# Layer 0's second norm as a node factor on ScalarE, and its keys, values and context moved beside the checks

## The chip, the core and the metric

The kernel runs on one core of one Trainium2 chip. The metric is the device time of one launch in microseconds (us), median over the runs shown; lower is better.

## The reference, cut to what matters

A graph of 3,125 nodes with 256 features and 103,125 edges, sorted by destination, goes through four layers. Each layer is a norm, a graph attention over the edges, a dense linear attention ("mix") over all nodes, and a feed-forward part. Only the front of layer 0 is touched by the change:

```python
xn = _layernorm(x)                                  # first norm
x = x + _L0_gnn_ref(xn, edge_index, ...) + _L0_mix_ref(xn[None], ...)[0]

def _L0_mix_ref(x, Wqkv, Wproj, bproj, ln_g, ln_b, Wg1, bg1, Wg2, bg2):
    q, k, v = split((x @ Wqkv))                     # 8 heads of 32
    k = softmax(k, axis=1)                          # over the nodes
    context = einsum('bnhd,bnhv->bhdv', k, v)
    out = einsum('bnhd,bhdv->bnhv', q, context)
    xn = (x - mean(x)) * rsqrt(var(x) + 1e-05) * ln_g + ln_b   # second norm, of a normed x
    hgate = gelu(xn @ Wg1 + bg1)
    gate = sigmoid(hgate @ Wg2 + bg2)
    return out * gate @ Wproj + bproj
```

The second norm is taken of rows that are normed already: their mean is 0 and their variance is v/(v + 1e-5), where v is the variance of the row of x. Its result is therefore the first norm's row times one number of that node.

## The kernel before, in words

Nodes lie in 25 tiles of 125 rows (`NT`, `TP`), and these in seven `GROUPS` of four or three tiles (500 or 375 nodes). `x` and the normed `xn` stay in SBUF by rows, `xT` holds the normed features transposed (two blocks of 128, `KC`).

`run` has these stages, one after the other:

1. **The begin** (`begin_layer`): `x` is loaded; for every group VectorE takes `bn_stats`/`bn_aggr` of each tile, ScalarE the square root, VectorE the reciprocal and the scaling (L613 to L619); TensorE transposes the tiles (L288), and ScalarE and VectorE copy them out to `xT` (L294, L296).
2. **The checks** (`prepare`): they establish whether the edges have the form that the fast path needs. `heads_i` (1.6 MB) is loaded, five comparisons over 3,224 numbers (L1381) give `at_i`, with which GpSimd gathers `seg` (L1387); VectorE works that into `lo` and `key` and writes both to `seg_d` in DRAM (L1392 to L1404); `dst_i` is compared (L1419 to L1428); TensorE multiplies `xT` with a 16-column matrix, and VectorE takes the largest and the least (`p_e`, `ends`, L1438, L1439). One number, `self.ok`, is the outcome, and all engines branch on it (L2479). Nothing behind the branch can run before it.
3. **The counts** (`counts`), with **layer 0's mix** beside them: `lo` and `key` are read back (`seg_in`), transposed by TensorE and copied out as `lo_t` and `key_t`. Then come 63 steps of ten groups of nodes. A step makes two one-hot tiles on VectorE (`oh_lo` L1515, `oh_key` L1518), 20 matmuls of them on TensorE (`p_cnt`, L1530), and ScalarE copies the counts out as bytes (`stage`, L1532). Every 250 nodes a stage goes to `count_d` in DRAM (L1536).
4. **The pairs** (`dense_pairs`): 25 x 8 x 2 passes that read `count_d` back as `a` (L1706) and bound VectorE and TensorE for over 300 us. The other layers follow.

The mix is a generator, `mix0_pieces`, which gives the control back after each piece of work; after each step of the counts as many pieces are issued as keep pace with `PIECES0` pieces over the 63 steps, and what is left follows behind the loop. The pieces before are: one for the weights and the bias (`nc.gpsimd.tensor_add` over all of `x`, L1557); 25 for the tiles' keys and values (four matmul instructions into `p_a` at L716, `ek` = exp of the keys at L1564 and `v` at L1566 on ScalarE, a column of ones by GpSimd at L1567, four matmul instructions into `p_ctx` at L1569); one that folds the context into the query weights (`ctxt`, `fold`, L1575 to L1587); then six for each group: second norm `xnn` (L613 to L619 again), transposes and scaling `xnnT` (L1599, L1600), `hg`, `gate`, the product with `fold` (L1616), the projection added to `x` (L1623); then 38 of `node_pieces`, which make the node tables `zs`, `bar`, `q_g` that the pairs use. That is 1 + 25 + 1 + 42 + 38 = 107.

The order of each engine's instructions is settled at build time by the tile framework: earlier emitted instructions have the higher priority, but one that its estimates hold ready may be put ahead of one that waits. [...] DMAs are issued from the queues of SP and ScalarE; GpSimd issues the gathers.

Of the kernel before, what the change touches and what calls it, by code (L numbers as in the profile page):

```python
# [10 lines left out]
F32 = mybir.dt.float32  # L11
# [30 lines left out]
KEYS = HI * GN  # L42
PIECES0 = 107
SC = 8
# [12 lines left out]
class Net:  # L57
# [546 lines left out]

    def layernorm(self, out, src, group=None):

        nc = self.nc
        w = self.norms
        for t0, nt in GROUPS if group is None else [group]:
            mv = w.tile([TP, 4, 2], F32, name="mv")  # L610
            for t in range(nt):
                st = w.tile([TP, nc.vector.BN_STATS_DIM], F32, name="bn_st")
                nc.vector.bn_stats(st, src[:, t0 + t, :])  # L613
                nc.vector.bn_aggr(mv[:, t, :], st)
            rstd = w.tile([TP, 4], F32, name="rstd")
            nc.scalar.activation(rstd[:, :nt], mv[:, :nt, 1], AF.Sqrt, bias=self.eps5[:TP], scale=1.0)
            nc.vector.reciprocal(rstd[:, :nt], rstd[:, :nt])
# [112 lines left out]
    def mix0(self, x, xn, xT):  # L730
        nc, tc = self.nc, self.tc
        with ExitStack() as s:
# [9 lines left out]
            bg1, bg2 = self.vec(c, "L0_mix_bg1", rows=64), self.vec(c, "L0_mix_bg2")  # L742
            bproj = self.row(c, "L0_mix_bproj", parts=1)
            gate = c.tile([P, KC, N], F32, name="gate")
# [53 lines left out]
            for t0, nt in GROUPS:  # L798
# [11 lines left out]
                for t in range(nt):  # L810
                    p = ps.tile([TP, C], F32, name="p_a")
                    self.mm(p, [(og[:, m, t * TP:(t + 1) * TP], wproj[:, m, :]) for m in range(KC)]
                            + [(self.ones[:1, :TP], bproj)])
                    nc.vector.tensor_add(x[:, t0 + t, :], x[:, t0 + t, :], p)
# [536 lines left out]
class Dense(Net):  # L1351
# [8 lines left out]
    def prepare(self, pool, xT):  # L1360
# [6 lines left out]
        with ExitStack() as s:  # L1367
# [65 lines left out]
            gw = self.gnn_weight(w, ps, "g0", 8)  # L1433
            ends = w.tile([16, 2, len(GROUPS)], F32, name="ends")
# [30 lines left out]
            nc.vector.tensor_mul(self.ok, ok[:, 0:1], ok[:, 2:3])  # L1465
        return self.ok

# [4 lines left out]
    def counts(self, pieces):  # L1472
# [5 lines left out]
        with ExitStack() as s:  # L1478
# [5 lines left out]
            with tc.tile_pool(name="cnti", bufs=1) as wi, tc.tile_pool(name="cntt", bufs=2, space=PSUM) as ps:  # L1484
                for i, name in enumerate(("lo_t", "key_t")):
# [57 lines left out]
    def mix0_pieces(self, x, xn, xT, nodes, c, w):  # L1543


        nc, tc = self.nc, self.tc
        with ExitStack() as s:
            ps = s.enter_context(tc.tile_pool(name="m0p", bufs=3, space=PSUM))
            ps1 = s.enter_context(tc.tile_pool(name="m0p1", bufs=1, space=PSUM))
            wqkv = self.weight(c, "L0_mix_Wqkv")  # L1550
            wproj = self.weight(c, "L0_mix_Wproj")
# [3 lines left out]
            bg1, bg2 = self.vec(c, "L0_mix_bg1", rows=64), self.vec(c, "L0_mix_bg2")  # L1555
            bproj = self.row(c, "L0_mix_bproj")
            nc.gpsimd.tensor_add(x, x, bproj[:, None, :].to_broadcast([TP, NT, C]))  # L1557
            p_ctx = [ps1.tile([P, P + 1], F32, name=f"p_ctx{m}") for m in range(KC)]
            yield
            for t in range(NT):  # L1560
                p = ps.tile([TP, 2 * C], F32, name="p_a")
                self.mm(p, [(xT[:, k, t * TP:(t + 1) * TP], wqkv[:, k, C:]) for k in range(KC)])
                ek = w.tile([TP, C], F32, name="ek", bufs=2)
                nc.scalar.activation(ek, p[:, :C], AF.Exp)  # L1564
                v = w.tile([TP, KC, P + 1], F32, name="v", bufs=2)
                nc.scalar.activation(v[:, :, :P], p[:, C:].rearrange("p (m f) -> p m f", m=KC), AF.Copy)  # L1566
                nc.gpsimd.memset(v[:, :, P], 1.0)  # L1567
                for m in range(KC):
                    nc.tensor.matmul(p_ctx[m], ek[:, m * P:(m + 1) * P], v[:, m, :], start=(t == 0), stop=(t == NT - 1))  # L1569
                yield  # L1570

            inv = w.tile([P, KC], F32, name="inv")
            ctxt = w.tile([P, KC, P], F32, name="ctxt")
            for m in range(KC):
                nc.vector.reciprocal(inv[:, m:m + 1], p_ctx[m][:, P:])  # L1575
                nc.vector.scalar_tensor_tensor(ctxt[:, m, :], p_ctx[m][:, :P], inv[:, m:m + 1], self.heads, op0=OP.mult, op1=OP.mult)
            fold = c.tile([P, KC, C], F32, name="fold")
            for k in range(KC):
                p = ps.tile([P, 512], F32, name="p_a")
                for m in range(KC):  # L1580
                    nc.tensor.transpose(p[:, m * P:(m + 1) * P], wqkv[:, k, m * P:(m + 1) * P], self.ident)
                wt = w.tile([P, C], F32, name="wq_t")
                nc.vector.tensor_copy(wt, p[:, :C])
                p = ps.tile([P, 512], F32, name="p_a")
                for m in range(KC):
                    nc.tensor.matmul(p[:, m * P:(m + 1) * P], wt[:, m * P:(m + 1) * P], ctxt[:, m, :], start=True, stop=True)
                nc.vector.tensor_copy(fold[:, k, :], p[:, :C])  # L1587
            yield
            for t0, nt in GROUPS:
                n = nt * TP  # L1590
                cs = slice(t0 * TP, t0 * TP + n)
                xnn = w.tile([TP, 4, C], F32, name="xnn")
                self.layernorm(xnn, xn[:, t0:t0 + nt, :], (0, nt))
                yield
                xnnT = w.tile([P, KC, 512], F32, name="xnnT")
                for k in range(KC):
                    p = ps.tile([P, 512], F32, name="p_a")
                    for t in range(nt):
                        nc.tensor.transpose(p[:, t * TP:(t + 1) * TP], xnn[:, t, k * P:(k + 1) * P], self.ident[:TP, :TP])  # L1599
                    nc.vector.tensor_scalar(xnnT[:, k, :n], p[:, :n], g[:, k:k + 1], b[:, k:k + 1], op0=OP.mult, op1=OP.add)  # L1600
                yield
# [864 lines left out]
    def run(self, x_in, out):  # L2466
# [195 lines left out]
```

## Time and profile before

| what | us |
|---|---|
| median of 3 runs (lowest, highest) | 5535.72 (5531.63, 5546.36) |
| the profiled execution: its own time | 5533.53 |
| its span in the trace | 5531.5 |
| begin and checks, until `ok` is written | 0 to 92.3 |
| from there to the first count matmul | 92.3 to 130.5 |
| the 63 steps | 130.5 to 384.7 |
| last copy of counts to the first matmul of the pairs | 384.7 to 408.2 |

The span is one execution on the core, and all stages are read from it. A row of windows gives the busy time of each engine in a stretch, with the number of instructions; "busy" of TensorE (PE) is the union of its matmuls. PEclk is the clock granted to it, as a share of full speed. In a group of instructions the columns are line, engine, operation, output <- inputs, shapes and count, then busy us and mean ns of one, then the engine's idle time before them and what ended it. A mean of a matmul is longer than the distance between two of them, since they overlap.

### The profile page before, as it was taken

What the parts mean: (1) busy time and instruction counts of PE and PEld (TensorE: products, weight loads), DVE (VectorE), ACT (ScalarE), POOL (GpSimd) and SP (SyncE); (2) the same over time, 40 slices, a digit from 0 to 9 for tenths busy, and PEclk for the clock granted to TensorE, in tenths of its full rate; (3) what the DMA queues carried; (4) which work ended last, traced back from release to release, by engine and by line L of the source; (5) the groups of instructions that cost most, each with busy time, mean ns of one, the idle gap of its engine ahead of it and who ended that gap; (6) DMA issues with size and microseconds to landing.
All of it is one profiled execution on the core that took longest, in us unless ns stands there. A gap on an engine that the chain in (4) does not pass through costs nothing. (4 is left out here: it accounts for less than half of the span.)

```text
span 5531.5 us, 66568 instructions
## 1 busy us (share of the span) xinstructions
PE 4813.9 (87%) x24758; PEld 2824.0 (51%) x24758; DVE 3733.4 (67%) x5901; ACT 1034.3 (19%) x1984; POOL 1041.6 (19%) x1185
## 2 busy tenths in 40 slices
PE   4978888879788899989889899979998878989878
PEld 2652234448645433368544433345565555655557
DVE  7789999985565699845333899932223888777753
ACT  2540010011142100110123000023333110333221
POOL 1000000004300000000001100000001777777743
PEclk7999999989899999999889999979999888999989
DMA  3462222232300011111000011120002556666645
GB/s 87 36 68 67 77 63 67 67 116 63 99 19 0 27 34 41 32 39 36 24 1 4 28 33 34 26 71 0 0 1 59 161 164 193 183 173 178 175 149 170
DMA packets 294339, 395.81 MB, mean 72 GB/s; under 512 B 124175, under 2 KB 228000, under 8 KB 293435
## 3 DMA queue, kind: packets, MB, share of 16 engines
q1 hardware_dynamic: 203408, 161.12, 12.7%
q0 software_dynamic: 52528, 167.17, 10.7%
q10 hardware_dynamic: 38072, 63.16, 3.6%
q8 instruction: 202, 3.31, 0.3%
q14 instruction: 129, 1.06, 0.1%
HBM read 345.14 MB, written 49.35 MB: 71 GB/s over the span
## 5 line engine op out<-in xcount | busy, mean ns | idle before, releaser
L1699 DVE SCALAR_TENSOR_TENSOR pt<-q_head,bar,a 128x750 f32<-128x750 f32 (+5 forms) x1200 | 1483.3, 1298 | 80.4 <-PE acc L1804 57.3
L1954 POOL DMA_INDIRECT z_edge<-tab,src_i x806 | 778.0, 965 | 266.9 <-issue 206.4
L1748 PE MATMUL acc<-pt,zs 128*64 128x500 f32 (+2 forms) x2800 | 591.1, 548 | 152.0 <-DVE pt L1699 127.2
L1799 PE MATMUL acc<-pt,zs 128*64 128x375 f32 (+2 forms) x3200 | 604.9, 501 | 25.4 <-DVE pt L1699 25.0
L2022 PE MATMUL p_acc<-z_edge,oh 128*125 128x264 f32 x2044 | 539.9, 425 | 91.7 <-DVE z_edge L2013 91.7
L2022 PEld LDWEIGHTS p_acc<-z_edge,oh 128*125 128x125 f32 x2044 | 419.8, 209 | 191.3 <-DVE z_edge L2013 101.2
L1748 PEld LDWEIGHTS acc<-pt,zs 128*64 128x64 f32 (+1 forms) x2800 | 244.4, 136 | 483.3 <-DVE pt L1699 328.7
L1799 PEld LDWEIGHTS acc<-pt,zs 128*64 128x64 f32 (+1 forms) x3200 | 244.9, 136 | 362.0 <-issue 224.7
L1215 DVE SCALAR_TENSOR_TENSOR x<-p_y,sm,x 125x256 f32<-125x256 f32 x200 | 93.9, 484 | 427.0 <-PE p_y L716 427.0
L1804 PE MATMUL acc<-pt,zs 128*32 128x375 f32 (+2 forms) x3200 | 313.4, 497 | 0.0
L1850 PE MATMUL acc<-zs,pt 128*125 128x257 f32 x1250 | 275.7, 383 | 11.8 <-DMA a<-count_d 11.8
L1850 PEld LDWEIGHTS acc<-zs,pt 128*125 128x125 f32 x1250 | 234.8, 189 | 52.7 <-issue 14.6
L2013 DVE TENSOR_TENSOR z_edge<-z_edge,near_e 128x2112 f32<-128x2112 f32 (+1 forms) x101 | 236.5, 2342 | 17.4 <-ACT near_e L2005 17.4
L1210 ACT ACTIVATE h<-p_tr,bn 128x500 f32<-128x500 f32 (+1 forms) x224 | 161.5, 722 | 357.6 <-PE p_tr L716 357.6
L716 PE MATMUL p_y<-w_L_ffn_Wo,h 128*125 128x256 f32 x800 | 203.7, 387 | 0.0
L1699 DVE SCALAR_TENSOR_TENSOR pt<-q_all,bar,a 128x500 f32<-128x500 f32 (+3 forms) x175 | 119.0, 682 | 122.9 <-PE acc L1850 120.4
L716 PE MATMUL p_tr<-h,w_L_ffn_W 128*128 128x500 f32 (+1 forms) x448 | 191.6, 551 | 7.8 <-ACT h L1210 4.7
L2362 POOL CAST one_e<-one 125x96 bf16<-125x96 f32 (+1 forms) x2 | 2.1, 1049 | 1013.5 <-DVE one L653 1013.5
L716 PE MATMUL p_tr<-xT,w_L_ffn_W 128*128 128x500 f32 (+1 forms) x448 | 190.0, 547 | 0.0
L1804 PEld LDWEIGHTS acc<-pt,zs 128*32 128x32 f32 (+1 forms) x3200 | 85.0, 109 | 203.0 <-issue 201.7
L716 PEld LDWEIGHTS p_y<-w_L_ffn_Wo,h 128*125 128x125 f32 x800 | 144.9, 187 | 73.4 <-ACT h L1210 27.1
L1967 DVE TENSOR_TENSOR hot<-row,near 125x1024 f32<-125x1024 int16 (+1 forms) x149 | 157.6, 1083 | 4.5 <-DMA row<-dst_row 2.9
(513 smaller groups left out, 6696.0 us busy)
## 6 DMA issues: line engine op xcount, KB each, us to landing
row<-dst_row SPq DMA_DIRECT2D x101, 224.0 KB
a<-count_d SPq DMA_DIRECT2D x96, 203.1 KB
a<-count_d SPq DMA_DIRECT2D x96, 187.5 KB
a<-count_d SPq DMA_DIRECT2D x144, 93.8 KB
ef<-in_edge_s SPq DMA_DIRECT2D x101, 128.0 KB
z_edge<-tab,src_i POOLq DMA_INDIRECT x806
count_d<-stage SPq DMA_DIRECT2D x12, 781.2 KB
q_head<-q_g ACTq DMA_DIRECT2D x24, 375.0 KB
```

The source lines that it names most:

```text
L716: self.nc.tensor.matmul(p, a, b, start=(i == 0), stop=(i == len(pairs) - 1))
L1210: nc.scalar.activation(o[:, m, :n], p[:, :n], AF.Relu, bias=b[:, e, m:m + 1], scale=g[:, e, m:m + 1])
L1215: nc.vector.scalar_tensor_tensor(x[:, t0 + t, :], q, wf[:, t, e:e + 1], x[:, t0 + t, :], op0=OP.mult, op1=OP.add)
L1699: self.nc.vector.scalar_tensor_tensor(pt[:K, :n], q, bar, a[:K, :n], op0=OP.max, op1=OP.mult)
L1748: nc.tensor.matmul(acc[64 * i:64 * i + 64, :b1 - b0], zs[:K, t, z:z + 64], pts[i][:K, b0:b1], start=(t == 0), stop=(t == NS - 1))
L1799: nc.tensor.matmul(acc[i // 2][64 * (i % 2):64 * (i % 2) + 64, b, :b1 - b0], zs[:K, t, i * W:i * W + 64], pts[i][:K, b0:b1], **st)
L1804: nc.tensor.matmul(acc[2][32 * i:32 * i + 32, b, :b1 - b0], zs[:K, t, z:z + 32], pts[i][:K, b0:b1], **st)
L1850: nc.tensor.matmul(acc[i], pt[:K, i * TP:(i + 1) * TP], zs[:K, t, :C + 1], start=(t == 0), stop=(t == NS - 1))
L1954: nc.gpsimd.indirect_dma_start(out=zs[i][:, j, :], out_offset=None, in_=table, in_offset=bass.IndirectOffsetOnAxis(ap=src[:, c0 + j:c0 + j ...
L1967: nc.vector.tensor_tensor(hots[i, t][:, q0 * 256:q1 * 256], rows[i][:, q0 * 256:q1 * 256], node[:, t:t + 1].to_broadcast([TP, (q1 - q0) * ...
L2013: nc.vector.tensor_mul(zh, zh, weight[:, :, :, None].to_broadcast([P, n, H, D + 1]))
L2022: nc.tensor.matmul(acc[t], ohs[i, t][:, k - a, :], zs[i][:, k - c0, :HW], start=(k == cols[t][0]), stop=(k == cols[t][1] - 1))
```

## The change

The begin, the checks and the first half of the mix become one function, `begin`; `prepare` turns into a generator with two stops. The second norm's statistics are not taken any more: `layernorm` is given `again`, in which it leaves the factor of each node, and `mix0_pieces` multiplies by it on ScalarE; `xnnT` is made on ScalarE too. The bias is added in `begin`. `fold` goes through DRAM (`fold_d`) from one stage to the other. `bproj` also goes out of `mix0`, which runs only in the general branch.

```diff
-PIECES0 = 107
+PIECES0 = 69
 def layernorm(self, out, src, group=None, again=None):
             nc.scalar.activation(rstd[:, :nt], mv[:, :nt, 1], AF.Sqrt, bias=self.eps5[:TP], scale=1.0)
+            if again is not None:
+                twice = w.tile([TP, 4], F32, name="twice")
+                nc.scalar.activation(twice[:, :nt], mv[:, :nt, 1], AF.Sqrt, bias=self.eps10[:TP], scale=1.0 + 1e-5)
+                nc.vector.reciprocal(twice[:, :nt], twice[:, :nt])
+                nc.vector.tensor_mul(again[:, t0:t0 + nt], twice[:, :nt], rstd[:, :nt])
...
 def prepare(self, pool, xT):
...                                    (gathers of seg)
+            yield
...                                    (seg to lo, key, found; dst)
+            yield
-            p_f = ps.tile([1, 2], F32, name="p_f")
+            p_f = ps.tile([1, 2], F32, name="p_e")
...                                    (p_e, ends, w_k, ok)
+    def begin(self, pool, x, xn, xT):
+        self.fold_d = self.dram.tile([P, KC * C], F32, name="fold_d")
...                                    (pools: c0w bufs=2; PSUM c0t 2, c0p 2, c0c 1)
+            checks = self.prepare(pool, xT)
+            next(checks)
+            wqkv = self.weight(c, "L0_mix_Wqkv")
+            p_ctx = [ps1.tile([P, P + 1], F32, name=f"p_ctx{m}") for m in range(KC)]
+            self.again = pool.tile([TP, NT], F32, name="again")
+            self.layernorm(xn, x, GROUPS[0], self.again)
+            for i, (t0, nt) in enumerate(GROUPS):
+                self.transposed(pst, xT, xn, groups=[GROUPS[i]])
+                if i + 1 < len(GROUPS):
+                    self.layernorm(xn, x, GROUPS[i + 1], self.again)
+                if i == 2:
+                    next(checks)
+                for t in range(t0, t0 + nt):
...                                    (p_a, ek, v, ones, p_ctx: as in mix0_pieces before)
+            bproj = self.row(c, "L0_mix_bproj")
+            nc.gpsimd.tensor_add(x, x, bproj[:, None, :].to_broadcast([TP, NT, C]))
...                                    (inv, ctxt, fold: as in mix0_pieces before)
+            nc.sync.dma_start(self.fold_d, fold.rearrange("p k f -> p (k f)"))
+            for _ in checks:
+                pass
 def counts(self, pieces):
-            ps = s.enter_context(tc.tile_pool(name="cntp", bufs=3, space=PSUM))
+            ps = s.enter_context(tc.tile_pool(name="cntp", bufs=4, space=PSUM))
 def mix0_pieces(self, x, xn, xT, nodes, c, w):
-            ps = s.enter_context(tc.tile_pool(name="m0p", bufs=3, space=PSUM))
-            ps1 = s.enter_context(tc.tile_pool(name="m0p1", bufs=1, space=PSUM))
-            wqkv = self.weight(c, "L0_mix_Wqkv")
+            ps = s.enter_context(tc.tile_pool(name="m0p", bufs=4, space=PSUM))
-            bproj = self.row(c, "L0_mix_bproj")
-            nc.gpsimd.tensor_add(x, x, bproj[:, None, :].to_broadcast([TP, NT, C]))
...                                    (25 pieces of keys and values, one of the context: gone)
             fold = c.tile([P, KC, C], F32, name="fold")
+            nc.sync.dma_start(fold.rearrange("p k f -> p (k f)"), self.fold_d)
             yield
...
-                self.layernorm(xnn, xn[:, t0:t0 + nt, :], (0, nt))
+                for t in range(nt):
+                    nc.scalar.activation(xnn[:, t, :], xn[:, t0 + t, :], AF.Copy, scale=self.again[:, t0 + t:t0 + t + 1])
...
-                    nc.vector.tensor_scalar(xnnT[:, k, :n], p[:, :n], g[:, k:k + 1], b[:, k:k + 1], op0=OP.mult, op1=OP.add)
+                    nc.scalar.activation(xnnT[:, k, :n], p[:, :n], AF.Identity, bias=b[:, k:k + 1], scale=g[:, k:k + 1])
 def run(self, x_in, out):
-        self.begin_layer(x, xn, xT)
-        ok = nc.values_load(self.prepare(pool, xT)[0:1, 0:1], min_val=0, max_val=1)
+        self.begin(pool, x, xn, xT)
+        ok = nc.values_load(self.ok[0:1, 0:1], min_val=0, max_val=1)
```

The pieces after are 1 + 42 + 38 = 81, of which 69 are spread over the 63 steps and the last twelve follow behind the loop.

More of the change, by code (lines that the diff above doesn't have):

```diff
@@ L603, in experts, with layernorm @@
         return t
-    def layernorm(self, out, src, group=None):
+    def layernorm(self, out, src, group=None, again=None):
         nc = self.nc
@@ L742, in mix0 @@
             bg1, bg2 = self.vec(c, "L0_mix_bg1", rows=64), self.vec(c, "L0_mix_bg2")
-            bproj = self.row(c, "L0_mix_bproj", parts=1)
             gate = c.tile([P, KC, N], F32, name="gate")
@@ L811, in mix0 @@
                     p = ps.tile([TP, C], F32, name="p_a")
-                    self.mm(p, [(og[:, m, t * TP:(t + 1) * TP], wproj[:, m, :]) for m in range(KC)]
-                            + [(self.ones[:1, :TP], bproj)])
+                    self.mm(p, [(og[:, m, t * TP:(t + 1) * TP], wproj[:, m, :]) for m in range(KC)])
                     nc.vector.tensor_add(x[:, t0 + t, :], x[:, t0 + t, :], p)
@@ L1428, in prepare @@
             nc.vector.tensor_reduce(found[:, 1:2], above, AX.X, OP.add)
-            p_f = ps.tile([1, 2], F32, name="p_f")
+            yield
+            p_f = ps.tile([1, 2], F32, name="p_e")
             nc.tensor.matmul(p_f, self.ones[:, 0:1], found, start=True, stop=True)
-            gw = self.gnn_weight(w, ps, "g0", 8)
+            gw = self.gnn_weight(w, ps, "g0", 8, "p_e")
             ends = w.tile([16, 2, len(GROUPS)], F32, name="ends")
@@ L1465, in prepare @@
             nc.vector.tensor_mul(self.ok, ok[:, 0:1], ok[:, 2:3])
-        return self.ok
+    def begin(self, pool, x, xn, xT):
+        nc, tc = self.nc, self.tc
+        self.fold_d = self.dram.tile([P, KC * C], F32, name="fold_d")
+        with ExitStack() as s:
+            c = s.enter_context(tc.tile_pool(name="c0", bufs=1))
+            w = s.enter_context(tc.tile_pool(name="c0w", bufs=2))
+            pst = s.enter_context(tc.tile_pool(name="c0t", bufs=2, space=PSUM))
+            ps = s.enter_context(tc.tile_pool(name="c0p", bufs=2, space=PSUM))
+            ps1 = s.enter_context(tc.tile_pool(name="c0c", bufs=1, space=PSUM))
+            checks = self.prepare(pool, xT)
[11 more added lines that the diff above has]
+                for t in range(t0, t0 + nt):
+                    p = ps.tile([TP, 2 * C], F32, name="p_a")
+                    self.mm(p, [(xT[:, k, t * TP:(t + 1) * TP], wqkv[:, k, C:]) for k in range(KC)])
+                    ek = w.tile([TP, C], F32, name="ek")
+                    nc.scalar.activation(ek, p[:, :C], AF.Exp)
+                    v = w.tile([TP, KC, P + 1], F32, name="v")
+                    nc.scalar.activation(v[:, :, :P], p[:, C:].rearrange("p (m f) -> p m f", m=KC), AF.Copy)
+                    nc.gpsimd.memset(v[:, :, P], 1.0)
+                    for m in range(KC):
+                        nc.tensor.matmul(p_ctx[m], ek[:, m * P:(m + 1) * P], v[:, m, :], start=(t == 0), stop=(t == NT - 1))
+            bproj = self.row(c, "L0_mix_bproj")
+            nc.gpsimd.tensor_add(x, x, bproj[:, None, :].to_broadcast([TP, NT, C]))
+            inv = c.tile([P, KC], F32, name="inv")
+            ctxt = c.tile([P, KC, P], F32, name="ctxt")
+            for m in range(KC):
+                nc.vector.reciprocal(inv[:, m:m + 1], p_ctx[m][:, P:])
+                nc.vector.scalar_tensor_tensor(ctxt[:, m, :], p_ctx[m][:, :P], inv[:, m:m + 1], self.heads, op0=OP.mult, op1=OP.mult)
+            fold = c.tile([P, KC, C], F32, name="fold")
+            for k in range(KC):
+                p = ps.tile([P, 512], F32, name="p_a")
+                for m in range(KC):
+                    nc.tensor.transpose(p[:, m * P:(m + 1) * P], wqkv[:, k, m * P:(m + 1) * P], self.ident)
+                wt = w.tile([P, C], F32, name="wq_t")
+                nc.vector.tensor_copy(wt, p[:, :C])
+                p = ps.tile([P, 512], F32, name="p_a")
+                for m in range(KC):
+                    nc.tensor.matmul(p[:, m * P:(m + 1) * P], wt[:, m * P:(m + 1) * P], ctxt[:, m, :], start=True, stop=True)
+                nc.vector.tensor_copy(fold[:, k, :], p[:, :C])
+            nc.sync.dma_start(self.fold_d, fold.rearrange("p k f -> p (k f)"))
+            for _ in checks:
+                pass
@@ L1555, in mix0_pieces @@
             bg1, bg2 = self.vec(c, "L0_mix_bg1", rows=64), self.vec(c, "L0_mix_bg2")
-            bproj = self.row(c, "L0_mix_bproj")
[L1557 to L1576, printed above, removed]
-            fold = c.tile([P, KC, C], F32, name="fold")
[L1578 to L1587, printed above, removed]
+            fold = c.tile([P, KC, C], F32, name="fold")
+            nc.sync.dma_start(fold.rearrange("p k f -> p (k f)"), self.fold_d)
             yield
```

## The prediction

> **What bounds the kernel now.** Only the first 408 us are touched, so I read the table of windows first, for who is busy when.
>
> ```profile
> 0.00:60.00 60.00, 18.22 (x69) 11.21 (x70) 48.99 (x123) 6.94 (x15) 8.65 (x62) 0.74 0.45 108
> 60.00:120.00 60.00, 22.72 (x61) 7.93 (x58) 43.85 (x97) 8.54 (x21) 15.10 (x7) 0.71 0.32 89
> 120.00:180.00 60.00, 56.36 (x401) 38.70 (x402) 42.16 (x39) 36.36 (x85) 4.46 (x21) 0.95 0.38 32
> 240.00:300.00 60.00, 56.62 (x361) 37.13 (x362) 51.20 (x58) 33.23 (x56) 0.00 (x0) 0.94 0.54 37
> ```
>
> The columns are length, PE, weight loads, DVE, ACT, POOL, PE clock. Begin and checks (to 92.3) belong to VectorE: 49 us of the first 60, with PE at 18. In the counts PE is busy 94%, VectorE 70 to 85%. The same question by groups of instructions, for the startup of the counts (93 to 131 us):
>
> ```profile
> L1557 POOL TENSOR_TENSOR x<-x,r_L_mix_bproj 125x6400 f32<-125x6400 f32 x1 | 13.7, 13682 | 12.8 <-DMA r_L_mix_bproj<-in_L_mix_bproj 12.8
> L1518 DVE TENSOR_TENSOR oh_key<-key_t,is_key 128x2520 bf16<-128x2520 bf16 x2 | 11.7, 5892 | 3.5 <-ACT key_t L1497 3.5
> L1569 PE MATMUL p_ctx<-v,ek 125*128 125x129 f32 x16 | 3.5, 359 | 7.5 <-POOL v L1567 7.5
> ```
>
> The bias addition holds GpSimd 13.7 us; behind it waits the memset of `v`, behind that `p_ctx` on PE (7.5 us), and two `oh_key` take 11.7 us instead of 2.9. So the first count matmul comes at 130.5. And for the steps (131 to 384 us):
>
> ```profile
> L1530 PE MATMUL p_cnt<-oh_key,oh_lo 128*128 128x125 bf16 x1245 | 91.6, 226 | 5.7 <-DVE oh_key L1518 4.5 <-ACT stage L1532 0.4 <-ACT zs L1665 0.4
> L1515 DVE TENSOR_TENSOR oh_lo<-lo_t,is_lo 128x2560 bf16<-128x2560 bf16 x60 | 89.3, 1489 | 30.5 <-PE p_cnt L1530 29.5
> L1518 DVE TENSOR_TENSOR oh_key<-key_t,is_key 128x2520 bf16<-128x2520 bf16 x60 | 87.8, 1464 | 0.0
> ...
> L716 PE MATMUL p_a<-w_L_mix_Wqkv,xT 128*125 128x512 f32 x74 | 35.6, 600 | 0.0
> ...
> L1569 PE MATMUL p_ctx<-v,ek 125*128 125x129 f32 x84 | 14.0, 290 | 1.6 <-ACT v L1566 1.0
> ```
>
> VectorE waits 29.5 us for PE to free one-hot buffers, PE only 5.7 before the counts: PE bounds the steps. The timeline gives the distance between two 512-column passes with the clock up, and the end of the stage:
>
> ```profile
> 125.70 0.19 PEld L716 LDWEIGHTS p_a<-w_L_mix_Wqkv,xT 128*125 128x125 f32 x1 [0.41 <-issue]
> ...
> 126.13 0.19 PEld L716 LDWEIGHTS p_a<-w_L_mix_Wqkv,xT 128*125 128x125 f32 x1 [0.24 <-issue]
> ...
> 400.94 12.88 SPq L1706 DMA_DIRECT2D a<-count_d  x5
> ...
> 408.15 7.04 PE L1748 MATMUL acc<-pt,zs 128*64 128x500 f32 x20 [24.32 <-DMA a<-count_d]
> ```
>
> 0.43 us a pass; and the pairs start 23.5 us after the last counts (384.7), because the last DMA to `count_d` has to land first.
>
> [...] The windows show 0.50 from 35 to 55 us, and 1.00 in the steps.
>
> **Part 1, the begin grows.** To PE goes: per tile four passes at 0.43 plus 0.61 for the four `p_ctx` (timeline, 129.13) = 2.33 us, for 25 tiles 58; fold 2.4 (rows L1581, L1586: 0.8 + 1.6). Its own there: transposes 11.2, of which I count 6 after 27 us; `p_e` 16 x 0.42 + 12 x 0.32 = 10.5 (0.43 scaled by columns); the rest 2.
> When can it start? `wqkv` (768 KB) now stands on SP behind `x` and `heads_i`: x 3.2 + heads 1.6 + dst 0.4 + wqkv 0.8 = 6.0 MB at the 259 to 272 GB/s of the windows 7 to 21 us is 23 us, plus some for the loads of `gw`: about 27 us. `x` is normed by then up to group 3 or so; `heads_i` lands about then too, its comparisons (17.8 + 1.8) have priority and delay the last groups, but PE has 9 us of work in every group.
> PE then ends at 27 + 6 + 58 + 2.4 + 10.5 + 2 = 106, and I add 2 for the clock to come up, and 5 for `ctxt`, copies and the chain to `ok` (2.6 in the trace, from 89.66). So `ok` at **113 instead of 92.3: +21**.
> VectorE isn't the bound: about 70 us now (windows to 93), plus 7 x 2 x 0.17 for the factor and 2.6 for the context = 75 from 7 us. It even loses a wait: `at_i` is ready some 10 us earlier, and the 7.4 us until `seg` lands are filled with norms. ScalarE gets 25 x 2 x 0.39 = 19.5, 7 x 0.3 for the second roots and a pair of table loads (2.6) wherever exp and sqrt alternate, at most 18: 40 of 85 us.
> GpSimd: 25 memsets, the five gathers (7.2 us) and the bias (13.7) share one list; a memset behind one of the latter holds `p_ctx` for up to that time less two tiles ahead (4.7), so 0 to 12 us, in which `p_e` can run on PE. I take 0. `bproj`'s load on ScalarE's queue, `fold_d`'s write on SP (0.26 MB) and its load after the branch cost nothing as long as VectorE or PE work: `fold` is wanted five pieces later. Bounds: +8 (PE's moved work in gaps that I don't see, `wqkv` at 20 us) to +40 (both POOL waits, all table loads).
>
> **Part 2, the startup of the counts shrinks.** Gone are the bias, the 25 `bn_stats` (9.6, which ran while VectorE waited for `key_t` anyway, so worth nothing), the load of `wqkv` and 26 passes plus 16 `p_ctx` in front of the last `seg_in` transposes. What stays is the chain: ten loads, two at a time, about 4 us each (99.2, 101.5, 106.6 in the timeline), `key_t` the sixth, then 3 us of one-hots: 18 to 22 us after the branch. I take 20 instead of 38.2: with the 1 us to the branch **-17** (-12 to -20).
>
> **Part 3, the steps shrink.** PE: windows 131 to 384 sum to 241.8; minus 35.6, 14.0 and 2.4 is 190, minus seven node tiles that go behind the loop (25.6/24 each) 182. VectorE: two one-hots 1.40 apart by the timeline, 63 steps 175; gate products, additions to `x` and `es` 18: 193. Its `xnn` (7.3) and `xnnT` (9.7) go to ScalarE as 25 x 0.40 and 14 x 0.63 (rows like L1611: 675 and 570), 19 us, for `ek`, `v` and their table loads that go (21); it stays at 143 of 210. So the bound changes from PE to VectorE, with PE 6% behind. PE reached 95% of 253.5; I give VectorE 92%, since both lists are in order: 193/0.92 = 210. **-43** (-28, if the two go on waiting for each other, to -50, VectorE at 95%).
>
> **Part 4, the tail.** Twelve pieces now follow: PE and ScalarE 8 us, exps and scaling 11, against 23.5 us of the write to `count_d`. I count 0, at most +3 (the last `q_g` write stands behind that DMA on SP).
>
> **The sum**: +21 - 17 - 43 = -39 against the profiled execution's own 5533.5: 5494.5. The median lies 2.2 above that, inside the spread; I say 5496.
>
> **Rivals.**
> *The begin hides the move.* PE idle 42 of the first 60 us speaks for it; against it that most of it lies before `wqkv` lands. With +5: 5480.
> *The steps don't follow.* In-order lists keep VectorE waiting for `p_cnt` as now (29.5 us): 193/0.84 = 230, -23 in place of -43: 5516, at the edge of what can be told.
> *Slower: keys and values run after the checks, not beside them.* PE's and GpSimd's lists are in order. If the first `v` memset is put behind the gathers, or the tiles behind `p_e` matmuls that wait for VectorE's reductions (now up to 80 us), PE sits. The moved 60 us plus the context then follow at 92: begin +72, and with -12 and -28 this is +32: 5568. It decides against the change once the first tile starts later than about 80 us, and clearly past 100. Against it: PE's list is built with readiness in view, and norms come before the gathers' result.
> *The change does less than it says*: the factor needs no more than 7 x 4 small instructions, and nothing else of the norm remains; I see no room for this.
>
> **How the numbers follow.** A measurement here can tell 0.3% (16.6 us) from no change. Main case, 5480 to 5512: 0.62, faster. Hidden: 0.15, faster. Steps that don't follow, or a begin at +40: 0.17, about a third of it faster, the rest the same or just slower. Keys and values after the checks: 0.06, slower. Faster 0.83, same 0.11, slower 0.06. The range 5468 to 5522 leaves out the far ends of the bounds together.
>
> **What would show it.** `ok` written at 105 to 125 us, with PE over 80% busy from 27 us on (right) or idle there behind `v` or `p_e` (rival). First count matmul some 20 us after the branch; `oh_key` never above 1.5 us there. In the steps VectorE at over 90% and PE's wait for `oh_key` above 10 us, VectorE's wait for `p_cnt` below 10. The last `stage` to the pairs still 23.5 us. If the steps still take 235 us or more with VectorE waiting for PE, part 3 was wrong; if `ok` comes after 140 us, part 1 was.

## The result, and the profile after

The changed kernel takes **5523.45 us** (median of 22 runs, 5514.09 to 5534.61), the kernel before 5534.98 in 22 runs taken with it (5526.73 to 5546.36). The ratio is **0.9979, interval 0.9973 to 0.9986**: a gain of 11.5 us, 0.2%, where 39 were forecast. The whole interval lies below 1, so the gain is clear of the noise; it is less than a third of the one forecast, and the time lies above the range of 5468 to 5522. The profiled execution took 5527.73 us, its span 5525.7.

In the windows of the changed kernel (same stretches and columns as before: length, PE, weight loads, VectorE (DVE), ScalarE, GpSimd, clock, DMA share, GB/s) the begin now has PE at work, 29 of the first 60 us and 47 of the next 60. The third stretch is mostly begin and startup. In the last one, in the steps, VectorE has 57.9 of 60, where it had 51.2.

```profile
0.00:60.00 60.00, 29.28 (x90) 15.69 (x91) 46.64 (x124) 18.09 (x38) 10.65 (x71) 0.86 0.55 132
60.00:120.00 60.00, 47.41 (x172) 24.40 (x170) 17.59 (x29) 15.24 (x42) 15.73 (x19) 0.89 0.09 28
120.00:180.00 60.00, 44.81 (x227) 22.58 (x227) 33.51 (x53) 24.33 (x52) 2.38 (x3) 0.80 0.21 51
240.00:300.00 60.00, 56.76 (x504) 43.21 (x503) 57.88 (x54) 44.20 (x85) 0.00 (x0) 1.00 0.69 54
```

Four marks, all starts of an instruction, cut the front in the parts of the forecast. The startup is from `ok` to the first count matmul, the steps from there to the last copy to `stage`, the tail from there to the first matmul of the pairs.

| part | before | after | measured | forecast |
|---|---|---|---|---|
| begin: `ok` at | 92.1 | 136.2 | +44.1 | +21 (+8 to +40) |
| startup | 38.4 | 29.9 | -8.5 | -17 (-12 to -20) |
| steps | 253.9 | 194.3 | -59.6 | -43 (-28 to -50) |
| tail | 23.7 | 28.2 | +4.5 | 0 (to +3) |
| first matmul of the pairs at | 408.1 | 388.6 | **-19.5** | -39 |

All four parts lie outside their bounds, the steps on the good side, the others on the bad one. The marks are of one profile each, and the medians are of 22 runs each: what separates -19.5 at the pairs from -11.5 in the medians lies behind the pairs (last experiment).

**The begin.** The timeline of the changed kernel (start, duration, engine, line, operation, in brackets the idle time before it and what ended it) shows the keys and values starting at 29.2 and PE stopping twice:

```profile
29.19 5.75 PE L722 MATMUL p_a<-w_L_mix_Wqkv,xT 128*125 128x512 f32 x8
...
52.27 0.89 PE L288 MATMUL p_tr<-ident,xn 125*128 125x125 f32 x3 [8.10 <-DVE xn L625]
...
69.36 0.68 PE L1506 MATMUL p_ctx<-v,ek 125*128 125x129 f32 x4
...
71.81 0.68 PE L1506 MATMUL p_ctx<-v,ek 125*128 125x129 f32 x4
...
79.08 13.66 POOL L1508 TENSOR_TENSOR x<-x,r_L_mix_bproj 125x6400 f32<-125x6400 f32 x1 [6.34 <-DVE xn L625]
...
92.84 2.09 PE L1506 MATMUL p_ctx<-v,ek 125*128 125x129 f32 x8 [12.02 <-POOL v L1504]
94.72 3.62 PE L722 MATMUL p_a<-w_L_mix_Wqkv,xT 128*125 128x512 f32 x4
...
102.77 0.55 DVE L294 COPY xT<-p_tr 128x375 f32<-128x375 f32 x1 [23.77 <-PE p_tr L288]
```

First, 8.1 us: the transposes of the fifth group stand in PE's list ahead of the next tiles, and wait for a norm that VectorE does behind the five comparisons (3.55 us each). Second, 12.0 us: the bias addition took its place in GpSimd's list ahead of the memsets of the last tiles' `v`; `p_ctx` waits for a memset of 0.1 us. The addition itself waited 6.3 us for the last norm, which stands in VectorE's list behind the work on `seg` (63.2 to 77.3), and in that time the memsets waited behind it, so that PE had only 1.7 us of work left when the addition began. PE, ScalarE and VectorE stand still with it: VectorE's next copy waits for a transpose that stands in PE's list behind that `p_ctx` (23.8 us). Four passes then take 3.62 us instead of 1.88 (the granted clock is 0.53 from 92.8 to 98.6, and 1.00 from 35 to 44). A tile takes 2.45 us, from `p_ctx` to `p_ctx` (69.36 and 71.81).

**The startup.** The two `oh_key` are back at 1.47 us each (groups of the stretch 137 to 166), since the addition is gone from there. They are ready at 157.8, 21.6 us after `ok`:

```profile
L1580 DVE TENSOR_TENSOR oh_key<-key_t,is_key 128x2520 bf16<-128x2520 bf16 x2 | 2.9, 1468 | 7.9 <-ACT key_t L1559 7.9
```

But PE's list has all `seg_in` transposes and the mix of the first group of nodes ahead of the first count (timeline):

```profile
164.65 0.38 PE L1557 MATMUL p_t<-ident,seg_in 125*128 125x125 f32 x2
164.86 1.01 PE L722 MATMUL p_a<-xT,fold 128*128 128x500 f32 x2
165.71 0.59 PE L722 MATMUL p_a<-w_L_mix_Wproj,gate 128*125 128x256 f32 x2
166.14 2.08 PE L1592 MATMUL p_cnt<-oh_key,oh_lo 128*128 128x125 bf16 x31
```

**The steps.** In the groups of 166 to 361 us VectorE's wait for `p_cnt` has gone from 29.5 to 4.4 us, and PE's wait for `oh_key` from 4.5 to 2.6. Both work nearly through: VectorE is busy 186 of the 195 us, PE 184. That VectorE sets the length is not seen here; e7_move_alone shows it, where more work for VectorE makes the steps longer.

```profile
L1592 PE MATMUL p_cnt<-oh_key,oh_lo 128*128 128x125 bf16 x1250 | 90.8, 228 | 2.9 <-DVE oh_key L1580 2.6 <-ACT stage L1594 0.2
L1577 DVE TENSOR_TENSOR oh_lo<-lo_t,is_lo 128x2560 bf16<-128x2560 bf16 (+1 forms) x61 | 89.8, 1472 | 4.7 <-PE p_cnt L1592 4.4
L1580 DVE TENSOR_TENSOR oh_key<-key_t,is_key 128x2520 bf16<-128x2520 bf16 (+1 forms) x61 | 88.4, 1450 | 0.0
```

**The tail.** In ScalarE's list the exponential `bar`, which the scaling of `zs` comes after, stands behind the issue of a load of `q_head` (timeline):

```profile
376.77 0.36 ACTq L1764 DMA_DIRECT2D q_head<-q_g  x1
377.18 0.37 ACT L1698 ACTIVATE bar<-es 128x200 f32<-128x200 f32 x1 [12.07 <-DMA count_d<-stage]
...
378.43 0.99 DVE L1704 TENSOR_TENSOR zs<-zs,es 128x800 f32<-128x800 f32 x1
...
386.49 5.16 DVE L1729 SCALAR_TENSOR_TENSOR pt<-q_head,bar,a 128x1500 f32<-128x1500 f32 x3
...
388.59 3.85 PE L1778 MATMUL acc<-pt,zs 128*64 128x500 f32 x8 [23.95 <-DMA q_head<-q_g]
```

ScalarE's wait of 12.1 us ends with the last write to `count_d`; then VectorE scales `zs` from 378.4 to 386.5 and goes on without a gap to `pt`, from which the first matmul is made. So the last work before the pairs is the scaling, though the profile puts the wait of PE down to `q_head`. In the kernel before, VectorE had scaled from 384.1 to 392.1, while that write was under way, and `pt` waited for `a` alone:

```profile
406.31 1.78 DVE L1699 SCALAR_TENSOR_TENSOR pt<-q_head,bar,a 128x1500 f32<-128x1500 f32 x1 [13.94 <-DMA a<-count_d]
```

### The profile page after: what moved, and what is told of

Same layout as the page of the kernel before. It is cut to its first block, busy times and chain, and to the rows that moved or that the text cites. A ratio compares the mean times of both kernels' runs of the same rounds, so it can differ in the third digit from the quotient of the medians.

```text
span 5525.7 us, 66520 instructions
## 1 busy us (share of the span) xinstructions
PE 4829.1 (87%) x24758; PEld 2828.2 (51%) x24758; DVE 3696.6 (67%) x5819; ACT 1053.6 (19%) x2023; POOL 1042.0 (19%) x1185
## 5 line engine op out<-in xcount | busy, mean ns | idle before, releaser
L1729 DVE SCALAR_TENSOR_TENSOR pt<-q_all,bar,a 128x500 f32<-128x500 f32 (+3 forms) x175 | 119.0, 682 | 122.9 <-PE acc L1880 120.6
```

What stands on the lines that cost most here:

```text
L1729: self.nc.vector.scalar_tensor_tensor(pt[:K, :n], q, bar, a[:K, :n], op0=OP.max, op1=OP.mult)
```

## The experiments

**The theory**: the change does to the work what was forecast, and half of its worth is lost in the begin to the order of the lists, where one waiting instruction holds all behind it. **The rival**: the begin has no room for the moved work, and a stall that is removed comes back elsewhere. All kernels differ from the changed one unless another is named; marks as in the table above, each from one profile.

| kernel | `ok` | startup | steps | tail | pairs at | median | ratio to before (interval) |
|---|---|---|---|---|---|---|---|
| after_again | 136.9 | 29.9 | 193.5 | 27.6 | 387.9 | 5525.66 | 0.9976 (0.9967 to 0.9986) |
| before_again | 92.0 | 38.8 | 252.8 | 23.7 | 407.3 | 5535.43 | 1.0001 (0.9992 to 1.0010) |
| e1_ones_once | 122.4 | 31.6 | 192.5 | 28.8 | 375.3 | 5501.16 | 0.9935 (0.9918 to 0.9952) |
| e2_norms_first | 133.7 | 31.2 | 194.1 | 27.7 | 386.7 | 5522.16 | 0.9972 (0.9960 to 0.9983) |
| e3_both | 134.3 | 30.0 | 193.4 | 27.3 | 385.0 | 5510.23 | 0.9956 (0.9939 to 0.9972) |
| e8_copies_act | 117.0 | 31.8 | 192.0 | 28.6 | 369.4 | 5499.41 | 0.9932 (0.9916 to 0.9949) |
| e9_checks_early | 102.3 | 38.1 | 193.6 | 26.6 | 360.6 | 5496.64 | 0.9925 (0.9906 to 0.9943) |
| e10_with_seg_in | 102.8 | 25.7 | 201.3 | 29.2 | 359.0 | 5491.07 | 0.9919 (0.9900 to 0.9939) |
| e4_seg_in_10 | 136.8 | 16.6 | 201.3 | 29.4 | 384.1 | 5512.16 | 0.9951 (0.9935 to 0.9968) |
| e5_pieces_81 | 136.7 | 31.8 | 204.5 | 19.1 | 392.1 | 5524.49 | 0.9979 (0.9969 to 0.9989) |
| e6_norm_alone | 92.4 | 41.6 | 249.1 | 22.9 | 406.0 | 5537.21 | 1.0004 (0.9995 to 1.0013) |
| e7_move_alone | 135.2 | 31.4 | 207.6 | 28.7 | 402.9 | 5528.50 | 0.9986 (0.9979 to 0.9992) |

### e1_ones_once: no memset in the loop

```diff
+            vs = [c.tile([TP, KC, P + 1], F32, name=f"v{i}") for i in range(2)]
+            for v in vs:
+                nc.gpsimd.memset(v[:, :, P], 1.0)
...
-                    v = w.tile([TP, KC, P + 1], F32, name="v")
+                    v = vs[t % 2]
-                    nc.gpsimd.memset(v[:, :, P], 1.0)
```

> The column of ones is set once in two fixed v tiles, so that no GpSimd memset stands in the loop over the tiles. Theory (the begin is late because GpSimd's list and PE's list are in order: a memset behind the 13.66 us bias addition holds p_ctx, PE idle 12.0 us from 81): that wait is gone, ok is written at about 122 instead of 136.2, and everything to the first matmul of the pairs comes 14 us earlier (388.6 to about 375); the time is some 14 us shorter than the changed kernel's, ratio to the kernel before about 0.9955. Rival (the stall only moves: DVE was idle from 79 to 102 too, so the next thing that PE's list holds is as late): ok within 3 us of 136, ratio 0.998.

Measured: `ok` at 122.4, the pairs at 375.3, both as the theory had them. The median (of four runs) is 22 us below the changed kernel's, not 14, and the ratio of 0.9935 lies below the 0.9955 expected: the 9 us beyond the pairs' 13.3 come from behind the pairs, where the edit changes nothing. The addition stands where it stood and takes as long, and the tiles run past it (timeline):

```profile
79.69 13.71 POOL L1510 TENSOR_TENSOR x<-x,r_L_mix_bproj 125x6400 f32<-125x6400 f32 x1 [19.35 <-DVE xn L625]
...
82.25 0.71 PE L1508 MATMUL p_ctx<-v,ek 125*128 125x129 f32 x4
82.81 1.88 PE L722 MATMUL p_a<-w_L_mix_Wqkv,xT 128*125 128x512 f32 x4
84.64 0.71 PE L1508 MATMUL p_ctx<-v,ek 125*128 125x129 f32 x4
```

So one memset of 0.1 us behind the wrong neighbour cost the change 13 to 14 us. A tile now takes 2.39 us: in the changed kernel the memset was on its path too.

### e2_norms_first and e3_both: the norms ahead of the comparisons

```diff
             next(checks)
+            self.again = pool.tile([TP, NT], F32, name="again")
+            for g in GROUPS:
+                self.layernorm(xn, x, g, self.again)
...
-                if i + 1 < len(GROUPS):
-                    self.layernorm(xn, x, GROUPS[i + 1], self.again)
```

e3_both has the edit of e1_ones_once as well.

> All seven groups' norms are written ahead of the comparisons and of the first tile's keys and values. Theory: PE's wait of 8 us at 44 to 52 (transposes of group 4 behind norms that VectorE does after the five comparisons) goes, and with it some of the alternations of the exp and sqrt tables, but at_i is ready 10 us later, so the gathers too; the stall at the bias addition stays: ok at 126 to 132 instead of 136.2. Rival (what PE gains there it loses waiting for the gathers, seg and the reductions): ok 136 to 142. Time against the changed kernel: -4 to -10 by the theory, 0 to +6 by the rival.

> Both edits: the column of ones set once, and all norms ahead of the comparisons. Theory: with both stalls gone the begin is near the sum that the prediction made (27 us + PE's own work): ok at 112 to 118 instead of 136.2, first matmul of the pairs at about 367, time some 18 to 24 us shorter than the changed kernel's. Rival (what remains behind the last tile, p_e and the reductions, is set by seg and the gathers): ok not before 128.

Measured: e2_norms_first has `ok` at 133.7, between the two; the first stall is gone, and `p_ctx` now waits for the memset twice, 7.0 us behind the addition and 5.4 behind the gathers. In e3_both it is at 134.3 where 112 to 118 was expected; the number is the rival's, and 12 us worse than e1_ones_once alone. PE had no stall up to 62 us, and then a longer one (timeline of e3_both):

```profile
69.70 1.49 DVE L1397 CAST rel<-seg 125x1280 f32<-125x1280 int32 x1 [10.71 <-DMA seg<-in_segments,at_i]
...
83.30 0.67 DVE L294 COPY xT<-p_tr 128x500 f32<-128x500 f32 x1
...
84.02 3.77 PE L722 MATMUL p_a<-w_L_mix_Wqkv,xT 128*125 128x512 f32 x4 [21.02 <-DVE xT L294]
```

VectorE had its norms done early, so the next in its list was the reduction of `seg`, which waits 10.7 us for the gathers and then works 13.6; a copy to `xT` of 0.67 us stands behind it, and PE waits for that copy 21.0 us. The rival's reason, work behind the last tile, isn't what the trace shows. It is again a small instruction behind a waiting one, on another engine.

### e8_copies_act: the copies to ScalarE

```diff
-                elif (i + k) % 2:
+                elif (i + k) % 2 and not act:
...
-                self.transposed(pst, xT, xn, groups=[GROUPS[i]])
+                self.transposed(pst, xT, xn, groups=[GROUPS[i]], act=True)
```

> All norms first and the column of ones set once, as in e3_both, and the copies of the transposes to xT in the begin all on ScalarE instead of half of them on VectorE. In e3_both PE waited 21.0 us (62.5 to 84) for a copy on VectorE that stood in its list behind the reduction of the gathered segments (10.7 us wait for seg, then 13.6 us of work). Theory (the begin is a matter of what stands behind what in the lists): that wait goes, PE works through from about 28 us, ok at 111 to 116 instead of 134.3, first matmul of the pairs at 362 to 367, ratio 0.9915 to 0.993. Rival (PE then waits for the reductions, the gathers or ScalarE): ok not before 124.

Measured: `ok` at 117.0, 17.3 us earlier than in e3_both and just past the theory's 116. From 28.9 to 82 us PE runs without a gap. What is left is one stall of 6.75 us (timeline):

```profile
36.38 13.73 POOL L1509 TENSOR_TENSOR x<-x,r_L_mix_bproj 125x6400 f32<-125x6400 f32 x1 [31.86 <-DVE xn L625]
39.70 11.27 DVE L1432 TENSOR_TENSOR col_lo<-col_lo,col_hi 128x806 f32<-128x806 f32 x1
...
88.90 0.19 PE L1436 MATMUL p_e<-found,ones 128*1 128x2 f32 x2 [6.75 <-DVE found L1421]
```

PE's list has `p_f`, a sum over `found`, ahead of the last tiles. The second line is one reason why `found`, which comes out of the gathered `seg`, is late: with all norms early, GpSimd's addition now runs beside the comparisons, and VectorE's product of two tensors, which took 0.99 us in the changed kernel, takes 11.27 between two of them; `at_i` is ready at 63 us instead of 51.

### e9_checks_early: the end of the checks ahead of the last tiles

```diff
+                if i == len(GROUPS) - 1:
+                    for _ in checks:
+                        pass
                 for t in range(t0, t0 + nt):
...
-            for _ in checks:
-                pass
```

with `p_f` behind the `p_e`s; on top of e8_copies_act.

> e8_copies_act, and the last part of the checks (p_e, its reductions, p_f behind them) written ahead of the last group's keys and values, so that these and the fold run beside the reductions. In e8_copies_act PE waited 6.7 us for p_f, and ok came 5 us after the last p_e. Theory: ok at 102 to 107, PE's last matmul of the begin at 109 to 113 (28.9 + 60 of keys and values + 2 of transposes + 10.5 of p_e + 6 of fold and small ones, with a few us of waits for the reductions), first count matmul at 141 to 145 instead of 148.8, first matmul of the pairs at 362 to 366. Rival (p_e then waits for VectorE, which is busy with the segments to 89): PE's last at 116 or later, no gain.

Measured: `ok` at 102.3, the first count at 140.4, the pairs at 360.6, each at the early end of the theory or just ahead of it. PE goes from 28.5 to 108.8 with 3.3 us of waits (timeline, two of them):

```profile
89.31 4.79 PE L722 MATMUL p_e<-xT,gw_g 128*16 128x500 f32 x12 [1.90 <-DVE ends L1443]
...
108.11 0.71 PE L1528 MATMUL p_a<-ctxt,wq_t 128*128 128x128 f32 x4 [0.29 <-DVE wq_t L1525]
...
140.36 1.83 PE L1594 MATMUL p_cnt<-oh_key,oh_lo 128*128 128x125 bf16 x27
```

So the order of the lists alone had held the begin up, and nearly all of its waits could be taken out. The rival keeps a part: stalls did come back elsewhere, in e2_norms_first and e3_both, and the begin isn't free room, since PE's own work ends at 108.8, 16.7 us after `ok` in the kernel before. The startup of 38.1 us counts from `ok`, which now comes 6.5 us before PE's last matmul of the begin; from that matmul it is 31.5.

### e4_seg_in_10 and e10_with_seg_in: ten buffers for ten loads

```diff
-                        x = wi.tile([TP, SEG], F32, name="seg_in", bufs=2)
+                        x = wi.tile([TP, SEG], F32, name="seg_in", bufs=10)
```

> The ten loads of seg_in at the startup of the counts have ten buffers instead of two, so that all are under way at once. Theory (the startup of 29.9 us is a chain of five pairs of loads of about 4 us each with transposes between them): startup 15 to 18 us, first count matmul at 151 to 154 instead of 166.1, all later marks 12 us earlier if the steps keep their 194.6 us; ratio to the kernel before about 0.9957. Rival ([...]the one-hots wait for key_t alone): startup 27 us or more.

> e9_checks_early with ten buffers for the ten loads of seg_in. Theory: startup 15 to 18 us instead of 30, but 7 us of pieces then go into the steps (as e4_seg_in_10 had it: 201 against 194.6), so the first matmul of the pairs comes 4 to 7 us earlier than in e9_checks_early, at 356 to 361; ratio to the kernel before 0.990 to 0.992. Rival (no gain left): the pairs within 2 us of e9_checks_early.

Measured: in e4_seg_in_10 the startup is 16.6 us, as the theory had it. In PE's list nothing of the mix is left ahead of the counts; PE waits for the last loads of `seg_in`, and the first count for ScalarE's `key_t` (timeline):

```profile
151.33 1.07 PE L1557 MATMUL p_t<-ident,seg_in 125*128 125x125 f32 x4 [2.82 <-DMA seg_in<-seg_d]
153.42 2.89 PE L1592 MATMUL p_cnt<-oh_key,oh_lo 128*128 128x125 bf16 x26 [1.02 <-ACT key_t L1559]
```

The pieces that had filled the startup are then in the steps, 201.3 us instead of 194.3, and the tail is 1.2 longer: 13.3 us won, 4.5 left at the pairs. The median gained 11.3, again with some 7 from behind the pairs. On top of e9_checks_early the same edit brought only 1.6 us at the pairs, within the rival's two, and the startup is 25.7 us, not 15 to 18, as PE's begin ends 6.8 us after `ok`. e10_with_seg_in still has the lowest median, **5491.07 us, ratio 0.9919 (0.9900 to 0.9939)**, though its interval overlaps those of e1, e8 and e9.

### e6_norm_alone and e7_move_alone: the two halves of the change

e6_norm_alone is the kernel before with `again` and ScalarE's `xnn` and `xnnT`; e7_move_alone takes these out of the changed kernel:

```diff
-                for t in range(nt):
-                    nc.scalar.activation(xnn[:, t, :], xn[:, t0 + t, :], AF.Copy, scale=self.again[:, t0 + t:t0 + t + 1])
+                self.layernorm(xnn, xn[:, t0:t0 + nt, :], (0, nt))
...
-                    nc.scalar.activation(xnnT[:, k, :n], p[:, :n], AF.Identity, bias=b[:, k:k + 1], scale=g[:, k:k + 1])
+                    nc.vector.tensor_scalar(xnnT[:, k, :n], p[:, :n], g[:, k:k + 1], b[:, k:k + 1], op0=OP.mult, op1=OP.add)
```

> The kernel before with the first half of the change alone: the second norm as a factor by node, scaled and shifted on ScalarE in the counts; keys, values, context and the bias addition stay in the counts. Theory (the steps are bound by PE, VectorE waits there anyway): steps 250 to 256 us as in the kernel before (254.2), first matmul of the pairs within 4 us of 408, ratio 0.999 to 1.0005. Rival (the two engines wait for each other in turn, so that VectorE's 17 us are worth something): steps 240 us or less, ratio below 0.9975.

> The changed kernel with the second half of the change alone: keys, values and context by groups beside the checks, but the second norm by VectorE in the counts as before. Theory (with the move, VectorE bounds the steps, at 97 to 99% of its work): ok as in the changed kernel (136 within 2 us), steps 194.6 + 17 = 209 to 214 us, first matmul of the pairs at 403 to 408, so that the move alone is worth nothing: ratio 0.999 to 1.001. Rival (the norm's work fits into gaps of VectorE): steps below 202 us.

Measured: the norm alone leaves the steps at 249.1, just under the theory's 250, and the time where it was (1.0004). In the groups of its steps VectorE's wait for `p_cnt` is longer than before, 36.0 us against 29.5: it was made faster, and PE bounds.

```profile
L1536 PE MATMUL p_cnt<-oh_key,oh_lo 128*128 128x125 bf16 x1250 | 91.0, 226 | 1.7 <-DVE oh_key L1524 1.1 <-ACT zs L1672 0.5
L1521 DVE TENSOR_TENSOR oh_lo<-lo_t,is_lo 128x2560 bf16<-128x2560 bf16 (+1 forms) x61 | 90.2, 1479 | 36.5 <-PE p_cnt L1536 36.0
```

The move alone takes the steps to 207.6, just under the theory's 209, and the time to 0.9986 (0.9979 to 0.9992), a small gain where none was expected. Here the wait has changed sides: PE waits 17.2 us for `oh_key`, VectorE 3.9.

```profile
L1591 PE MATMUL p_cnt<-oh_key,oh_lo 128*128 128x125 bf16 x1250 | 92.4, 231 | 18.2 <-DVE oh_key L1579 17.2 <-ACT stage L1593 0.7
L1576 DVE TENSOR_TENSOR oh_lo<-lo_t,is_lo 128x2560 bf16<-128x2560 bf16 (+1 forms) x61 | 90.2, 1479 | 3.9 <-PE p_cnt L1591 3.9
```

In the steps the move is worth 46.3 us, the norm after it 13.3, and the norm by itself 4.8. The begin and the tail take most of the move's gain back: at the pairs it has 5.2 us.

### e5_pieces_81: no pieces behind the loop

```diff
-PIECES0 = 69
+PIECES0 = 81
```

> The changed kernel with all 81 pieces in the steps and none behind the loop. Theory (the tail of 27.9 us against 23.5 comes from the pieces behind the loop, whose q_g write and q_head loads stand ahead of bar on their queues): tail 22.5 to 25 us, but steps longer by the 7 to 11 us of those pieces, since VectorE bounds them: first matmul of the pairs at 388 to 396 instead of 388.6, nothing gained. Rival (the steps have room for the pieces): pairs at 383 to 386.

Measured: the tail is 19.1 us, shorter than expected and than before; the steps are 204.5, ten longer. The pairs come at 392.1, and the time is that of the changed kernel. In the timeline the first pair waits for `count_d` itself, as in the kernel before:

```profile
392.14 3.78 PE L1778 MATMUL acc<-pt,zs 128*64 128x500 f32 x6 [19.43 <-DMA a<-count_d]
```

So the twelve pieces behind the loop cost about 9 us of tail and spare about 10 of steps.

### before_again and after_again: what one profile is worth

> The kernel before once more, unchanged, for the spread of one profile: from the first matmul of the pairs to the first p_acc of the edges the first profile has 3881.2 us, the changed kernel and its four variants 3887 to 3895; from the first to the last p_acc 1036.1 against 1033 to 1042. Theory (spread of a single profile): this one has 3885 to 3893. Rival (the changed kernels lose 6 to 13 us in stages whose instructions they share): again within 2 us of 3881. Ratio 1 within 0.001.

> The changed kernel once more, unchanged. Its first profile has the pairs 19.6 us earlier than in the kernel before, while the medians of 22 runs each lie 11.5 us apart; two profiles of the kernel before differ by 18 us from the pairs to the edges. Theory (the marks up to the pairs repeat, the stages behind them scatter): ok 135 to 138, pairs 387 to 390, and from the pairs to the end anything from 5123 to 5140. Rival (the pairs' mark itself scatters, and its mean is nearer 396): pairs at 392 or later.

Measured: the marks up to the pairs repeat within 1 us in both kernels. The kernel before has 3899.3 us from the pairs to the first `p_acc` of the edges this time, against 3881.2: neither the theory's 3885 to 3893 nor the rival's 3881, but 18 us of spread. So the difference of single profiles there says little. From the pairs to the end the changed kernel has 5137.7, after 5137.1.

Nearly all of the 18 us, 15.6, lies in one stretch, from the last pairs of layer 0 to the first of the next. Windows of just that stretch, in the first profile of the kernel before and in the second, show where:

```profile
1167.90:1893.30 725.40, 600.81 (x2527) 423.90 (x2526) 400.65 (x978) 171.72 (x338) 117.71 (x150) 0.91 0.18 55
1167.80:1908.80 741.00, 617.25 (x2527) 433.29 (x2526) 401.09 (x978) 171.78 (x338) 117.73 (x150) 0.88 0.18 54
```

The same 2,527 matmuls keep PE busy 16.4 us longer, at a granted clock of 0.88 in place of 0.91, and the other engines do the same work in the same time. Over all 14 profiles the traces' records of the granted clock give 584 to 633 us at half clock behind the pairs, and more of it goes with a longer way to the end (5123 to 5139 us; correlation 0.83). The two profiles of the kernel before are the ends of that range, and both of the changed kernel have 615.

The medians, less 2 us around the span and the pairs' mark, are steadier: 5125 to 5126 us behind the pairs for the kernel before, 5133 to 5136 for the changed one, and 5123 to 5134 in the ten variants, in no order that goes with an edit: e1_ones_once and e3_both have 5123 to 5124, e2_norms_first 5133.5, e9_checks_early 5134. Every profile has the same number of instructions on each engine there, 22,784 matmuls among them. So the granted clock goes with much of the spread between profiles. **Why the medians of two kernels differ by 8 us there stays open**: no run holds the clock fixed, and none shows why it is granted less in one execution than in another.

## Why the prediction was wrong, step by step

**The begin: the sum was right, the waits were not.** The work was well sized: 29.2 us for the first tile (27 said), 2.39 us a tile without the memset (2.33), and e9_checks_early with nearly no waits ends PE's begin at 108.8, where the sum had 106 and, as its author's estimate, 2 for the clock. Two sentences failed. "PE has 9 us of work in every group": true of a group of four tiles, but the comparisons were put between two groups' norms with 17.8 us, and PE waited 8.1. "A memset behind one of the latter holds `p_ctx` ... 0 to 12 us, in which `p_e` can run on PE. I take 0": the wait was 12.0, and no `p_e` on `xT` came before 119.0, since PE's list had them behind that `p_ctx`. That 12.0 is also the upper bound is chance. By the forecast's own working the addition can cost 13.7 less 4.7, that is 9.0, and the gathers 2.5; but PE was only 1.7 us ahead of the addition, not two tiles, and the gathers cost it 0.8. 113 + 2.2 for the start + 3.0 for the tiles + 8.1 + 12.0 is 138, against 136.2. The bound of +40 had GpSimd's waits in it and the value taken had not; the 8.1 behind the comparisons was in neither. For a wait that was seen, with its cause, in the kernel before (7.5 us, the same addition, the same memset), nothing was the wrong value. The bias went to the begin together with the keys and values, and so did the stall between them.

ScalarE's table loads were eight of 1.28 us, at the exponentials and square roots, together 10.3 us of the 18 at most that were counted (from 137 to 361 us they stand at `hg` and `gate`, none at `xnn`, `xnnT` or `stage`), and PE's waits for ScalarE in the begin are under 1 us in sum. "`at_i` is ready some 10 us earlier" was 3 (51.0 against 53.7), and the wait for `seg` was filled with norms only in part: VectorE stood 6.6 us, with the last norm behind that wait in its list.

**The startup: right chain, wrong end.** 20 us were said for the loads and one-hots, and the first `oh_key` were ready after 21.6. But the first count needs its turn in PE's list, and the freed room had been filled with a piece of the mix: 29.9. e4_seg_in_10 shows that two buffers made it so. This is 8.5 of the 19.5 us missed at the pairs.

**The steps: right mechanism, term too small.** PE ceased to be the bound, as said. The floors, 193 us for VectorE and 182 for PE, were close: the windows from 166 to 361 have 186 and 184 busy. The step that failed is the share: 92%, because PE's list was thought to hold VectorE up. It hardly did (4.4 us), and VectorE reached 95%, so the steps are 194.3 and not 210. This gave back 16 to 17 of what the begin and the startup lost, some 7 of them by VectorE's floor. PE's wait for `oh_key`, said to be above 10 us, is 2.6: the two engines are nearly even. e6_norm_alone and e7_move_alone show that the two halves of the change belong together here, and why each by itself does little.

**The tail.** 0 was taken, at most +3; it is +4.5. The forecast let the scaling of the pieces behind the loop run under the write to `count_d`, and named the `q_g` write as the risk. The scaling came behind that write instead. In e5_pieces_81, which has none behind the loop, `a` landed 5.4 us after its issue at 384.9; from the changed kernel's issue at 376.9 that would be 382.3 (an estimate), and `pt` began at 386.5, 4.2 us later. No run moves `bar` ahead of that load alone.

**Behind the pairs** 0 was taken, and 8 us were lost between the medians, for no cause shown. Without them the time would have been about 5515, inside the range and still 19 us above the value of 5496: that the range was missed is due to these 8 us as well, that the value was missed is due to the begin and the startup.

**Of the rivals**, the one that would have made it slower (keys and values after the checks) decides from a first tile at 80 us; it came at 29.2. The steps that don't follow were wrong the other way. e9_checks_early, another order of the same work, comes nearest to "the begin hides the move": `ok` at +10.2, and -47.5 us at the pairs.

## What to carry to other kernels

When work moves to an idle stretch, write down for each engine the order in which its list will stand there, and look for small instructions (a memset, a copy, a norm) behind long or waiting ones: here 0.1 us behind 13.7 cost 12, and 0.67 behind a gather cost 21. Taking one stall away is worth its length only if what stands next in the lists is free: of two such edits, one brought `ok` its full 14 us, and both together 2. Relief for an engine off the bound is worth little until the bound moves to it (here 4.8 us of steps alone, 13.3 after the move), so test the halves of a change against each other.

## What the runs showed of the hardware

**Two operands beside GpSimd.** In e8_copies_act the product of two 128x806 tensors on VectorE took 11.27 us, of which GpSimd added the bias for the first 10.4, and ended 0.9 us after the addition. The same instruction took 0.99 us in e3_both, where it came behind the addition; there its neighbour, also of two operands, fell beside it and took 7.23, again to 0.9 us after its end. The addition took 13.66 to 13.77 us in every place, with VectorE idle or busy, and the comparisons with one tensor operand took 3.56 to 3.57 us beside it, 3.55 to 3.57 without it. In the kernel before, the two `oh_key`, also of two operands, took 11.7 us in place of 2.9 from 113.6 on, and ended 2.7 us after the addition's end at 122.6. So in these three profiles the addition of 13.7 us held VectorE's work on two tensors to its end, and did not hold its comparisons.

**The clock.** The 0.50 that the forecast reads from 35 to 55 us in the kernel before is the granted clock, in a stretch in which PE was busy 1.0 of 20 us; over its steps (131 to 384) the mean is 0.99. In the changed kernel the four passes behind the stall of 12.0 us took 3.62 us, at a granted clock of 0.53, against 1.88 with the clock at 1.00: 1.7 us more, on top of the stall's length. Behind the 21.0 us in e3_both four passes took 3.77, with the clock at 0.52 from 80 to 90. Behind the pairs, where all kernels do the same work, the time at half clock differed by up to 49 us between two profiles of one kernel, and the time by 15.
